# Sums over edges for the first 256 nodes: row fetches from a DRAM table instead of a matrix product with counts

## The chip, the cores and the metric

The kernel runs on one core of a Trainium2 chip. Its time is the device time of one execution in microseconds (us). A time before or after is the median over several executions on the chip; one execution was also recorded by the hardware profiler, and the views below are of that one. Engines are named as the profile names them: PE is TensorE (PEld its loads of weights), DVE is VectorE, ACT is ScalarE, POOL is GpSimd, SP is the engine that starts most of the DMAs. L1773 is line 1773 of the kernel before the change.

## The reference

The input is 3125 nodes with 256 features and 103125 edges, sorted by destination (every node has an edge to itself). Four layers follow one another, each with a layer norm ahead of it and its input added behind it: a graph attention network of three layers, a mixture of experts, a layer that sums messages over edges, and a second mixture of experts. The change is in the third of them:

```python
def _L1_gnn_ref(x, W, M, edge_src, edge_dst):
    self_term = x @ W
    msg = x @ M
    agg = jax.ops.segment_sum(msg[edge_src], edge_dst, num_segments=x.shape[0])
    return jax.nn.relu(self_term + agg)
...
x = x + _L0_gnn_ref(_layernorm(x, axis=-1), src, dst, ...)
x = x + _L0_ffn_ref(_layernorm(x, axis=-1)[None], ...)[0]
x = x + _L1_gnn_ref(_layernorm(x, axis=-1), L1_gnn_W, L1_gnn_M, src, dst)
x = x + _L1_ffn_ref(_layernorm(x, axis=-1)[None], ...)[0]
```

## The kernel before

Nodes lie in 25 tiles of 128 (P is 128, NT is 25, D is 256). Early on, the edge lists are turned into a matrix of counts, 3125 sources by 3125 destinations, as bytes in SBUF. It is kept in 13 groups of destinations (GROUPS): twelve of 256 and a last one of 53. The attention layers and the sum layer all use it, so that a sum over edges becomes a product with the counts.

The attention's second layer also has a second way. For the first 512 destinations (class Apart, L2049) the sources of each node were listed, 38 to a node (OWN); nodes with more edges give the remainder to a shared tile of up to 128 heavy nodes with 20 places each (HEAVY). `ends` holds where each node's list begins and how long it is, `key` says which heavy place a node has, and `who` the source numbers, one column for each place. Each column is one indirect DMA on POOL that fetches 128 rows from a DRAM table (L2168), and DVE adds the rows (L2194). Those columns stand among the steps of the matrix product, at times that were written down by hand (`events`), and the block is issued under `tc.manual_schedule()` (L1526): there each engine takes its instructions in the order in which the code issues them. Elsewhere the scheduler of the framework orders each engine's instructions by a model of their times.

The sum layer is `dense_sum` (L1742). It has two phases.

- **Messages** (L1754 to L1762). In pieces of one to four tiles, `normalised` (L1723) makes the layer norm: statistics on DVE (L1728, L1729), the root on ACT (L1731), the scaling on DVE (L1735), two transposes on PE (L1738) and a copy on ACT into xnT (L1739). PE multiplies with M (L1760), and the message is kept as two numbers of reduced precision whose sum is the exact one: ACT casts the high part (L1761), DVE subtracts it for the rest (L1762).
- **Groups** (L1763 on). For each group of 256 destinations PE goes over 25 tiles of sources. At each of those steps ACT turns the bytes of the counts into numbers (`cr`, L1773, from a pool of four buffers; it also gives the sum of the row into `seen`, which at the end tells whether all edges were counted), and PE multiplies them with both halves of the messages, once for each of the group's two tiles (L1777). At the first step the self term x W is added into the same accumulators (L1780). When a group has ended, `back` finishes it during the next group, from step 8 on: for each tile ACT copies the low half out of PSUM (y, L1785), DVE adds the high half (L1786) and adds the clipped sum to x (L1787); then `normalised` makes the two tiles of xnT for the next layer. `back` stands at step 8 of the code; where its instructions come on each engine is the scheduler's decision, since this phase is not under manual_schedule.

After the sum layer the last mixture begins with the products of xnT (L1056).

Of the kernel before, what the change touches and what calls it, by code (L numbers as in the profile page):

```python
# [10 lines left out]
F32 = mybir.dt.float32  # L11
F16 = mybir.dt.float16
BF16 = mybir.dt.bfloat16
I32 = mybir.dt.int32
# [3 lines left out]
OP = mybir.AluOpType  # L18
# [1261 lines left out]
HELD = 64.0  # L1280

# [76 lines left out]
def dense_attention(tc, dram, counts, x_in, big, ident, eps, layers, src, dst, rows, high, make_router, over, count,  # L1358
# [11 lines left out]
    with tc.tile_pool(name="dw", bufs=1) as cp, tc.tile_pool(name="dwl", bufs=2) as wl, \  # L1370
# [3 lines left out]
        with tc.tile_pool(name="dp", bufs=6) as pmp, tc.tile_pool(name="ds", bufs=2) as sp, \  # L1374
# [12 lines left out]
            apart = Apart(tc, cp, dram, locator, *count, ident, top)  # L1387
# [332 lines left out]
    return expert  # L1720


def normalised(nc, wp, pp, x, t0, n, xnT, ident, eps):  # L1723

    mv = wp.tile([P, n, 2], F32, name="n_mv")
    for i in range(n):
        st = wp.tile([P, 6], F32, name="n_st")
        nc.vector.bn_stats(st, x[:, t0 + i])  # L1728
        nc.vector.bn_aggr(mv[:, i], st)  # L1729
    rstd = wp.tile([P, n], F32, name="n_rstd")  # L1730
    nc.scalar.activation(rstd, mv[:, :, 1], AF.Sqrt, bias=eps)  # L1731
    nc.vector.reciprocal(rstd, rstd)
    for i in range(n):
        xn = wp.tile([P, D], F32, name="n_xn")
        nc.vector.tensor_scalar(xn, x[:, t0 + i], mv[:, i, 0:1], rstd[:, i:i + 1], op0=OP.subtract, op1=OP.mult)  # L1735
        ps = pp.tile([P, KD, P], F32, name="ps_n")
        for k in range(KD):
            nc.tensor.transpose(ps[:, k], xn[:, k * P:(k + 1) * P], ident)  # L1738
        nc.scalar.copy(xnT[:, :, (t0 + i) * P:(t0 + i + 1) * P], ps)  # L1739


def dense_sum(tc, x, xnT, counts, ws, wm, ident, eps, total):  # L1742
# [6 lines left out]
    with tc.tile_pool(name="s1", bufs=1) as cp, tc.tile_pool(name="sb", bufs=4) as bp, \  # L1749
# [4 lines left out]
        msg = cp.tile([P, NT, 2, D], F32R, name="msg")  # L1754
        for t0, n in PIECES:
            normalised(nc, yp, tp, x, t0, n, xnT, ident, eps)
            for t in range(t0, t0 + n):
                ps = mp.tile([P, D], F32, name="ps_m")
                for k in range(KD):
                    nc.tensor.matmul(ps, xnT[:, k, t * P:(t + 1) * P], wm[:, k], start=(k == 0), stop=(k == KD - 1))  # L1760
                nc.scalar.copy(msg[:, t, 0], ps)  # L1761
                nc.vector.tensor_tensor(msg[:, t, 1], ps, msg[:, t, 0].bitcast(F32), op=OP.subtract)  # L1762
        later = []  # L1763
        for a, (c, n) in enumerate(GROUPS):
            edges = counts_of(counts, a)
            tiles = [(q, (c + q) // P, min(P, n - q)) for q in range(0, n, P)]
            n += n % 2
            acc = po.tile([P, 2, 2, D], F32, name="acc")
            for s in range(NT):
                if later and s == 8:  # L1770
                    later.pop()()
# [3 lines left out]
                for j, (q, t, r) in enumerate(tiles):  # L1775
# [3 lines left out]
                    for k in range(KD if s == 0 else 0):  # L1779
                        nc.tensor.matmul(acc[:r, j, 0], xnT[:, k, c + q:c + q + r], ws[:, k], start=False, stop=False)  # L1780

            def back(tiles=tiles, acc=acc):
# [5 lines left out]
                normalised(nc, yp, tp, x, tiles[0][1], len(tiles), xnT, ident, eps)  # L1788
            later.append(back)
        later.pop()()  # L1790
# [258 lines left out]
class Apart:  # L2049

    def __init__(self, tc, cp, dram, locator, before, every, ident, top):
# [3 lines left out]
        self.ends = cp.tile([P, FEW + 1, 2], F32, name="ends")  # L2055
        self.key = cp.tile([P, FEW], F32, name="heavy_key")
        self.width = sum(n for _, n in SLOTS_OF)
        self.who = cp.tile([P, self.width], I32, name="apart_who")
        self.table = dram.tile([N, ROW], F32, name="apart_rows")

    def save(self, sources, t, r):
        self.nc.sync.dma_start(self.table[t * P:t * P + r], sources.h[:r, t])
# [184 lines left out]
def routed(ctx: ExitStack, tc: tile.TileContext, i: dict, out: bass.AP, over):  # L2247
# [12 lines left out]
    with tc.tile_pool(name="counts", bufs=1) as kp:  # L2260
# [7 lines left out]
        expert = dense_attention(tc, dram, counts, i["x"], big, ident, eps, layers, i["src"], i["dst"], (rows0, rows),  # L2268
# [3 lines left out]
        with tc.tile_pool(name="s0", bufs=1) as sp:  # L2272
# [5 lines left out]
            dense_sum(tc, x, xnT, counts, ws, wm, ident, eps, over[:, 2:3])  # L2278
# [94 lines left out]
```

## Time and profile before

| | us |
|---|---|
| median of 14 executions (1865.08 to 1878.02) | 1868.56 |
| the profiled execution | 1870.27 |
| its span, from its first instruction to its last | 1868.5 |
| PE busy, of the span | 1768.1 (95%) |
| DVE busy | 1021.0 (55%) |
| ACT busy | 727.2 (39%) |
| POOL busy | 499.6 (27%) |
| sum layer: branch before it passed, first message product, first whole group, last cr | 1384, 1390, 1422, 1593 |
| products with the counts, L1777, in the layer | 625 of 404 ns, 158 busy |
| row fetches of the attention, L2168 | 172 of 1083 ns, 472 to 753 |

The page of the profile gives the busy time of each engine, the span in 40 slices, the chain of work that ended last, and the costliest groups of instructions. "Chain of waits" is that chain followed back from the last instruction: where an engine ran without waiting, its own work stands there. In the views of waits, "A <- B: 53.5, 17, 6.9" says that A's engine stood idle until B for 53.5 us in total, 17 times, at most 6.9. In a timeline each line has the start, the duration, the engine, the line of the code, the operation, what it writes and reads, its shapes and how many were merged; a bracket gives the idle time just before it and what ended it. Matmuls are pipelined, so one of 404 ns can start every 233 ns. The clock is the share of full speed that PE was granted.

### The profile page before, as it was taken

How to read it: one execution, taken by the hardware profiler on the slowest of the kernel's cores; microseconds unless marked ns; L12 is line 12 of the kernel's file. 1: busy time of each engine (PE TensorE's matmuls, PEld its weight loads, DVE VectorE, ACT ScalarE, POOL GpSimd, SP SyncE). 2: the span in 40 equal slices, each digit the busy share in tenths (PEclk: the TensorE clock that was granted, in tenths of full speed). 3: DMA queues.
4: the chain of work that ended last, by engine and by line, in shares of the span. 5: the costliest groups of instructions: out<-in, count | busy, mean ns of one | idle time of the engine just before them, and what ended most of it. 6: DMA issues, size and time to landing. Idle time of an engine off the chain costs nothing. (4 is left out here: it accounts for less than half of the span.)

```text
span 1868.5 us, 27219 instructions
## 1 busy us (share of the span) xinstructions
PE 1768.1 (95%) x9196; PEld 1379.9 (74%) x9196; DVE 1021.0 (55%) x2933; ACT 727.2 (39%) x2080; POOL 499.6 (27%) x634
## 2 busy tenths in 40 slices
PE   6999999999698988999999999999989999999997
PEld 4788888887586777788887866666668887455786
DVE  6888888875475757677777842222244222333221
ACT  3767667671011111122222331111127999454221
POOL 4210110000566766123333233333310000122121
PEclk9999999999898999999999999999999999999999
DMA  4111213757322332211111176877430000723884
GB/s 116 33 47 49 77 49 149 318 225 283 81 76 79 85 84 74 89 39 46 46 46 42 43 221 185 242 199 197 111 89 1 1 1 1 237 113 151 262 302 125
DMA packets 123716, 215.45 MB, mean 115 GB/s; under 512 B 14811, under 2 KB 86657, under 8 KB 123528
## 3 DMA queue, kind: packets, MB, share of 16 engines
q1 hardware_dynamic: 85860, 137.38, 22.0%
q0 software_dynamic: 24704, 56.84, 11.6%
q10 hardware_dynamic: 12994, 19.29, 3.2%
q8 instruction: 79, 1.29, 0.3%
q14 instruction: 79, 0.65, 0.1%
HBM read 122.54 MB, written 92.61 MB: 115 GB/s over the span
## 5 line engine op out<-in xcount | busy, mean ns | idle before, releaser
L1577 PE MATMUL acc<-big,pm 128*128 128x257 f32 x3400 | 799.7, 386 | 14.9 <-DVE pm L1574 9.5
L1577 PEld LDWEIGHTS acc<-big,pm 128*128 128x128 f32 x3400 | 635.0, 192 | 108.6 <-DVE pm L1574 14.9
L1574 DVE SCALAR_TENSOR_TENSOR pm<-tau,big,counts 128x256 f32<-128x256 f32 (+1 forms) x875 | 403.1, 480 | 123.9 <-PE acc L1577 98.7
L2168 POOL DMA_INDIRECT apart_row<-apart_rows,apart_who x172 | 186.4, 1083 | 104.7 <-issue 44.7
L1777 PE MATMUL acc<-msg,cr 128*128 128x512 f32 (+1 forms) x625 | 157.9, 403 | 0.1
L891 PE MATMUL ps_h<-xsT,w 128*128 128x384 f32 x448 | 147.3, 487 | 0.0
L1777 PEld LDWEIGHTS acc<-msg,cr 128*128 128x128 f32 (+1 forms) x625 | 114.7, 185 | 29.2 <-ACT cr L1773 1.2
L1773 ACT ACTIVATE cr<-counts 128x256 fp32r<-128x256 uint8 (+1 forms) x325 | 130.6, 402 | 13.9 <-PE acc L1777 6.9
L2034 ACT CAST counts<-acc_c 128x500 uint8<-128x500 f32 (+1 forms) x155 | 95.9, 677 | 94.5 <-PE acc_c L2024 94.3
L891 PEld LDWEIGHTS ps_h<-xsT,w 128*128 128x128 f32 x448 | 84.7, 190 | 58.0 <-issue 1.9
L1344 PE MATMUL ps_m<-we,yT 128*128 128x258 f32 (+1 forms) x248 | 72.1, 411 | 35.4 <-issue 24.6
L2009 DVE TENSOR_TENSOR ohk<-iota_k,key 128x2016 f16<-128x2016 f16 (+1 forms) x79 | 94.6, 1198 | 19.8 <-PE acc_c L2024 19.7
L894 ACT ACTIVATE silu<-ps_h 128x384 f32<-128x384 f32 x60 | 29.4, 490 | 170.4 <-PE ps_h L891 160.0
L1475 ACT ACTIVATE yT<-ps_m 128x256 f32<-128x256 f32 (+1 forms) x25 | 9.5, 378 | 218.6 <-PE ps_m L1473 104.9
L2003 ACT ACTIVATE ohs<-iota_s,low 128x128 f16<-128x128 f16 x286 | 94.0, 400 | 0.0
L1056 PE MATMUL ps_H<-big,t_w 128*128 128x512 f32 (+1 forms) x224 | 93.1, 552 | 0.8 <-ACT H L1058 0.5
L895 DVE TENSOR_TENSOR hid<-silu,ps_h 128x384 f32<-128x384 f32 x60 | 33.2, 554 | 104.0 <-PE ps_h L891 104.0
L911 POOL DMA_INDIRECT sums<-y,who x45 | 70.0, 1556 | 74.1 <-DVE y L909 66.1
L1184 PE MATMUL ps_y<-t_wd,hsT 128*128 x384 | 87.1, 379 | 0.4 <-ACT hsT L1232 0.4
L2024 PEld LDWEIGHTS <-ohs 128*128 128x128 f16 x1250 | 77.7, 98 | 10.9
L1344 PEld LDWEIGHTS ps_m<-we,yT 128*128 128x128 f32 (+1 forms) x248 | 45.0, 197 | 53.8 <-issue 28.1
L2024 PE MATMUL acc_c<-ohk,ohs 128*128 128x125 f16 x1250 | 84.5, 218 | 0.0
(424 smaller groups left out, 2246.1 us busy)
## 6 DMA issues: line engine op xcount, KB each, us to landing
rows<-empty SPq DMA_DIRECT2D x16, 2564.0 KB
big<-in_L_ffn_w_dram SPq DMA_DIRECT2D x36, 512.0 KB
w<-in_L_ffn_w_dram ACTq DMA_DIRECT2D x36, 512.0 KB
hs<-rows SPq DMA_DIRECT2D x23, 641.0 KB
rows<-empty SPq DMA_DIRECT2D x16, 516.0 KB
t_wd<-in_L_ffn_Wd_dram SPq DMA_DIRECT2D x8, 1024.0 KB
big<-in_L_ffn_Wd_dram SPq DMA_DIRECT2D x6, 1024.0 KB
xs<-rows SPq DMA_DIRECT2D x14, 387.0 KB
```

Source lines behind the costliest of these rows:

```text
L891: nc.tensor.matmul(ps, w[:, k, j * P:(j + 1) * P], xsT[:, k], start=(k == 0), stop=(k == KD - 1))
L1056: nc.tensor.matmul(ps[:, :n], a[:, k, j * P:(j + 1) * P], xnT[:, k, c:c + n], start=(k == 0), stop=(k == KD - 1))
L1344: nc.tensor.matmul(ps[:r], xT[:, k], w[:, k], start=(k == 0), stop=(k == KD - 1))
L1574: nc.vector.scalar_tensor_tensor(pm[:, :n], tau[:, :n], now.rho[:, of:of + 1], edges[:, of, :n], op0=OP.max, op1=OP.mult)
L1577: nc.tensor.matmul(acc[:r, j, :D + 1], pm[:, q:q + r], now.h[:, of, :D + 1], start=(s == 0), stop=(s == NT - 1))
L1773: nc.scalar.activation(cr[:, :n], edges[:, s, :n], AF.Copy, accum_out=seen[:, a * NT + s:a * NT + s + 1])
L1777: nc.tensor.matmul(acc[:r, j].rearrange("p h d -> p (h d)"), cr[:, q:q + r], msg[:, s].rearrange("p h d -> p (h d)"), start=(s == 0), stop ...
L2003: nc.scalar.activation(far[:, i], self.iota_s, AF.Abs, scale=-1.0, bias=self.low32[:, batch, i:i + 1])
L2009: nc.vector.tensor_tensor(to[:, i:tiles].rearrange("p t (x u) -> p t x u", u=2), iota.rearrange("p (x u) -> p x u", u=2)[:, None].to_broad ...
L2024: nc.tensor.matmul(acc[:, u], ohs[:, i], ohk[:, i, :KEYS], start=(t == 0), stop=(t == TW - 1))
L2034: nc.scalar.copy(to[:, :, d0 % PAIR:d0 % PAIR + whole * WIN].rearrange("p s (u d) -> p u s d", u=whole), acc[:, :whole])
L2168: nc.gpsimd.indirect_dma_start(out=row[:, j], out_offset=None, in_=self.table[:, :], in_offset=bass.IndirectOffsetOnAxis(ap=self.who[:, q ...
```

## The change

Group 0 of the sum layer, 256 destinations in two tiles, no longer goes through the product with the counts. Its sums follow the edges, with the lists that the attention made: `ends`, `key` and `who` are now kept in the pool of the counts (`kp`) until the sum layer has ended.

- Ahead of the messages DVE sums group 0's counts into `seen`, in five reductions; the room of those counts then holds six places for rows, and one-hots of the heavy nodes are made and transposed.
- After each tile's message, POOL adds the two halves and SP stores the row to a DRAM table (`save`).
- After the first of the remaining groups, `begin` issues six fetches. There are 96 in all: 20 columns of the heavy places, then 38 for each of the two tiles. DVE multiplies each row by a mask (`real`) and adds it (`slot`); behind a slot the fetch that is six further on is issued.
- When a tile's columns are done, PE multiplies the one-hots with the heavy sums and adds the self term (`finished`); at steps 19 and 4 `close` adds both, adds the clipped sum to x, and makes xnT.
- From the second remaining group on everything stands under `tc.manual_schedule()`. `back` is in two parts, at step 8 (the y copies, the sums, the statistics, the root and the scaling) and at step 16 (the transposes and the copies). Both are issued ahead of that step's cr.

The constants say at which step a row's sum is written into the order: the first after 8.5 us (ARRIVED), each further one after 1.26 (PACE), with 13.8 for a group (WHOLE), 11.7 for the first (FIRST) and 0.468 for a step (PART).

```diff
+SINGLE = 2
+FOLLOW = SLOTS_OF[:1 + SINGLE]
+PLACES = 6
+BACK, CLOSE = (8, 16), (19, 4)
+ARRIVED, PACE = 8.5, 1.26
+FIRST, WHOLE, PART = 11.7, 13.8, 0.468
...
+def normalised_steps(nc, wp, pp, x, t0, n, xnT, ident, eps):
...
+    for i in range(min(2, n)):
+        scaled(i)
+    yield
     for i in range(n):
-        xn = wp.tile([P, D], F32, name="n_xn")
-        nc.vector.tensor_scalar(xn, x[:, t0 + i], mv[:, i, 0:1], rstd[:, i:i + 1], op0=OP.subtract, op1=OP.mult)
+        if i >= 2:
+            scaled(i)
+        xn = held.pop(0)
         ps = pp.tile([P, KD, P], F32, name="ps_n")
...
+class Followed:
+    def __init__(self, tc, dram, apart, counts, cp, pp, ident):
...
+        for t in range(SINGLE):
+            hot = self.place()[:, :P]
+            nc.vector.tensor_scalar(hot, numbers, apart.key[:, t:t + 1], None, op0=OP.is_equal)
+            nc.tensor.transpose(ps[:, t], hot, ident)
+        nc.scalar.copy(self.back, ps)
...
+    def save(self, t, msg):
+        nc, row = self.nc, self.place()
+        nc.gpsimd.tensor_tensor(row, msg[:, t, 0].bitcast(F32), msg[:, t, 1].bitcast(F32), op=OP.add)
+        nc.sync.dma_start(self.table[t * P:(t + 1) * P], row)
+
+    def fetch(self, q):
+        row = self.place()
+        self.nc.gpsimd.indirect_dma_start(
+            out=row, out_offset=None, in_=self.table[:, :],
+            in_offset=bass.IndirectOffsetOnAxis(ap=self.apart.who[:, q:q + 1], axis=0))
+        return row
+
+    def events(self, finished):
...
+        def slot(q, first):
+            row, real = rows.pop(q), self.real[:, q:q + 1]
+            if first:
+                state["acc"] = self.cp.tile([P, D], F32, name="f_acc", bufs=3)
+                nc.vector.tensor_scalar(state["acc"], row, real, None, op0=OP.mult)
+            else:
+                nc.vector.scalar_tensor_tensor(state["acc"], row, real, state["acc"], op0=OP.mult, op1=OP.add)
+            if q + PLACES < total:
+                rows[q + PLACES] = self.fetch(q + PLACES)
...
-def dense_sum(tc, x, xnT, counts, ws, wm, ident, eps, total):
+def dense_sum(tc, dram, apart, x, xnT, counts, ws, wm, ident, eps, total):
+        for s in range(0, NT, WIN):
+            nc.vector.tensor_reduce(seen[:, s:s + WIN], counts_of(counts, 0)[:, s:s + WIN], AX.X, OP.add)
+        singles = Followed(tc, dram, apart, counts, cp, mp, ident)
...
+                singles.save(t, msg)
...
+        def finished(t, acc, hot, heavy):
+            ps = mp.tile([P, D], F32, name="ps_m")
+            nc.tensor.matmul(ps, hot, heavy, start=True, stop=False)
+            for k in range(KD):
+                nc.tensor.matmul(ps, xnT[:, k, t * P:(t + 1) * P], ws[:, k], start=False, stop=(k == KD - 1))
+
+            def close():
+                nc.vector.tensor_tensor(acc, acc, ps, op=OP.add)
+                nc.vector.scalar_tensor_tensor(x[:, t], acc, 0.0, x[:, t], op0=OP.max, op1=OP.add)
+                yield from normalised_steps(nc, yp, tp, x, t, 1, xnT, ident, eps)
+            steps = close()
+            closing.extend((q, lambda: next(steps, None)) for q in CLOSE)
+
+        begin, made = singles.events(finished)
+        order = ExitStack()
+        for g, (a, (c, n)) in enumerate(list(enumerate(GROUPS))[SINGLE // 2:]):
...
+            if g == 1:
+                begin()
+                order.enter_context(tc.manual_schedule())
             acc = po.tile([P, 2, 2, D], F32, name="acc")
             for s in range(NT):
-                if later and s == 8:
-                    later.pop()()
+                for step in [e for e in later if e[0] == s]:
+                    later.remove(step)
+                    step[1]()
+                if closing and closing[0][0] == s:
+                    closing.pop(0)[1]()
                 cr = bp.tile([P, PAIR], F32R, name="cr")
...
+                while g and made and made[0][0] <= (g, s):
+                    made.pop(0)[1]()
...
-                normalised(nc, yp, tp, x, tiles[0][1], len(tiles), xnT, ident, eps)
-            later.append(back)
-        later.pop()()
+                yield from normalised_steps(nc, yp, tp, x, tiles[0][1], len(tiles), xnT, ident, eps)
+            steps = back()
+            later.extend((q, lambda steps=steps: next(steps, None)) for q in BACK)
+        order.close()
+        while made:
+            made.pop(0)[1]()
+        for _, step in later + closing:
+            step()
```

## The prediction

> **What bounds the stage now.** I read the page's slices first (TensorE at nine tenths or more from 1400 to 1590 us, DMA idle there), then the chain of waits from 1370 to 1660 us, then busy time by stretch, then the timeline of one group. The sum layer's groups are a chain of TensorE work alone:
>
> ```profile
> 1558.32 0.86 PE acc L1780 x4
> 1559.19 0.23 PE acc L1777
> 1559.42 0.86 PE acc L1780 x4
> 1560.28 3.26 PE acc L1777 x14
> 1563.54 0.44 PE ps_n L1738 x4
> 1563.98 8.17 PE acc L1777 x35
> 1572.15 0.86 PE acc L1780 x4
> ```
>
> A group of 256 destinations repeats after 13.83 us (1572.15 - 1558.32): 50 message products at 0.233, eight passes of the self term (1.72), four transposes (0.44). So a step of one source tile is 0.466 us.
>
> ```profile
> 1440.00:1480.00 40.00, 40.00 (x180) 32.58 (x179) 10.36 (x33) 36.66 (x159) 0.00 (x0) 1.00 0.00 1
> 1400.00:1410.00 10.00, 10.00 (x53) 7.99 (x52) 9.54 (x36) 6.39 (x20) 0.00 (x0) 1.00 0.01 2
> ```
>
> Columns: stretch, then busy PE, PEld, DVE, ACT, POOL, clock, DMA share, GB/s. In the groups (first line) ACT is busy 36.7 of 40 us, only 8% short of becoming the bound. While messages are made (second line) DVE is busy 9.5 of 10. What ACT does between its conversions (cr, L1773) is the part that the change touches:
>
> ```profile
> 1572.43 0.35 ACT L1785 COPY y<-acc 128x256 f32<-128x256 f32 x1
> 1573.27 0.37 ACT L1785 COPY y<-acc 128x256 f32<-128x256 f32 x1 [0.49 <-DVE y L1786]
> 1575.55 0.28 ACT L1731 ACTIVATE n_rstd<-n_mv,eps 128x2 f32<-128x2 f32 x1
> 1575.74 0.40 ACT L1773 ACTIVATE cr<-counts 128x256 fp32r<-128x256 uint8 x1
> 1577.21 0.60 PE L1738 MATMUL ps_n<-ident,n_xn 128*128 128x128 f32 x4
> 1577.88 0.63 ACT L1739 COPY big<-ps_n 128x256 f32<-128x256 f32 x2
> ```
>
> From the first y copy to the end of the root is 3.40 us, because seven DVE operations stand between. Today three other cr (at 1573.54, 1574.67, 1575.14) go in between, and a fourth follows the root at once; those feed TensorE. The last two lines are the transposes and the copies that wait for them.
>
> **The parts.** The sum is against the profiled execution, 1870.27 us (span 1868.5, 1.77 outside it), 1.7 above the median of 1868.56.
>
> *(a) One group goes*, 13.83. *(b) TensorE work put back* for its two tiles: the spread of the shared rows, one fp32 256-column product of two passes (0.43), four self passes (0.86), two transposes (0.22) for each tile, and two transposes of the one-hots at the start: 2 x 1.51 + 0.22 = 3.24. Net **-10.6**.
>
> *(c) Ahead of the messages*, DVE gets five sums of group 0's counts (128x1280 uint8 to 128x5). No such row exists. The longest sum over full width is L1792 (325 elements, 0.491), a short one is L241 (32 elements, 0.186); their slope, 1.04 ns an element, makes 1.5 us of 1280, 7.5 for five. Masks and one-hots add 1.0 (L2110: 0.28 each). They stand first on DVE, are ready after the branch (1383.96), and statistics come behind them. Before the first 1.4 us and before the second another 1.4 DVE only waits for the loads, so 8.5 - 2.8 = **+5.7** arrives at the messages, where DVE has no slack. Bounds: 0 (placed in the idle time after 1415) to 8.5.
>
> *(d) The table.* 25 additions on POOL (L1545: 0.73 for the same shape, 18 us over a phase of 33) and 25 SP stores at 0.34 to issue, 8.5 us. POOL and SP have nothing else to do here. The last row is fetched only after the last store has landed, some 4.3 us after its issue (466.9 to 471.3 in the attention stage): **0**; without that cover, about 4.
>
> *(e) 96 fetches and 96 sums.* POOL issues one per 1.26 us (0.96 and 0.30), 121 us in all; the first row lands near 1430, the last near 1553, with the stage ending at 1593 or later. 96 sums at 0.40 a piece (starts of L2194 back to back) are 38 us on a DVE that is busy 10 of 40. Six places cover a landing of 3 us. **0**, up to +16 if rows come at the 1.63 us that the attention stage needed a row on average (751.8 - 472.1 over 172): then 156 us, and the end waits.
>
> *(f) Order of issue.* From the second group on, each engine keeps the order of the code. That code puts y copy, y copy and root at step 8 ahead of cr 8, and the two xnT copies at step 16 ahead of cr 16. The cr pool has four buffers, so when ACT reaches step 8 TensorE ends step 3. ACT then: cr 7 (0.46), copies and root (3.40 today with DVE free to reorder, some 3.6 in order), cr 8 until its sum is read (0.51): 4.6 us, against 4 x 0.466 = 1.87 that TensorE can live on. **Wait 2.7 us.** Behind the root stand all later cr, and TensorE waits for those. At step 16 no lead is possible at all: the copy needs the transposes and cr 16 stands behind the copy. From the transposes' start 1.30 to the end of the copies (1577.21 to 1578.51), 0.51 for cr, less 0.60 of transposes: **1.2**. Lead returns during the next self term. Ten full groups x 3.9 = 39, and 4 in the short last one, where the reserve is 4 x 0.26: **+43**. Bounds: 0 if ACT is not held, 55 if DVE is behind with row sums.
>
> *(g) The two followed tiles' closing*, at steps 19 and 4: root 0.3, transposes and copy 1.0, and 1.0 of lead lost for the following step 8, twice: **+4.6**; bounds 0 and 8.
>
> *(h) The clock.* Waits of that size have a second price in this trace:
>
> ```profile
> 581.08:584.49 3.41, 1.34 (x6) 0.87 (x5) 2.84 (x8) 0.00 (x0) 2.49 (x4) 1.00 0.34 90
> 584.49:587.90 3.41, 2.79 (x8) 1.66 (x6) 0.68 (x2) 0.00 (x0) 2.50 (x4) 0.50 0.39 109
> ```
>
> TensorE idled 2.07 us in the first stretch, and the next was granted half a clock. A wait of 2.29 (to 702.55) had the same follow, one of 2.95 (to 545.33) had none. Two of three, 11 waits, 1.7 us lost in 3.41 at half clock: **+11** to 12; I take 11, bounds 0 and 19.
>
> On this the Trainium skill, "TensorE: Matmul & The Clock Gate", Part 1, says that half rate is what an idle window of about 3.4 us brings. By it a wait of 2.7 would halve nothing and the sum would be 11 lower; the row disagrees, and the row decides.
>
> **Sum:** -10.6 + 5.7 + 43 + 4.6 + 11 = +53.7, so 1924 in a profiled execution and **1922** against the median. By the bounds of c, f, g and h at their likely sides (f 25 to 50, h 0 to 19) this case reaches from 1895 to 1945.
>
> **A precedent in the same trace.** The second attention layer keeps the order of issue too, with 172 row fetches. Its groups, by the reciprocal L1622, take 30.9 us on average (490.28 to 768.01, nine groups) and those of the third layer 23.82. In its waits from 515 to 770 us
>
> ```profile
> DVE lr L1351 <- ACT raw L1480: 53.5, 17, 6.9
> POOL apart_row L2168 <- DVE apart_acc L2194: 39.4, 20, 8.7
> ```
>
> DVE stood 17 times for 3.1 us behind an ACT result, and POOL waited for DVE, not for rows: order costs there, and fetches do not.
>
> **Rivals.**
>
> 1. *ACT is not held* (faster). If ACT still runs ahead at steps 8 and 16, only a to c remain: 1868.6 - 10.6 + 5.7 = 1864, or 1858 if the counts' sums are hidden. For it: ACT has 2 us to spare in a group, and y could start earlier. Against it: those 2 us cannot be used through four buffers, and L1351's waits show that order is kept. It decides where the wait per group falls below (10.6 - 5.7)/11 = 0.45 us. 0.22.
> 2. *Only the long step is partly held* (slower by less): DVE runs the statistics while ACT waits and the clock stays up; f of 10 to 25 and h of 0 give 1872 to 1895. 0.10.
> 3. *Rows set the pace.* If DVE waits for rows ahead of step 8, the root comes later by as much, and the groups go at the pace of 11 rows. At 1.63 a row that is 18 us a group, no more than case f has already; it adds to f only if rows need over 1.7 us. Together with half clocks throughout: 1945 to 1980. 0.06.
> 4. *The change saves nothing and costs nothing*, f near 5 (0.45 a group): within 0.2%, 3.7 us, about what a measurement of this kernel can tell from no change. 0.04.
>
> The likeliest, held ACT, has 0.58. The range 1862 to 1945 takes it in with case 2, case 4 and the half of case 1 that ends at 1862 to 1865; left out are 0.11 below and 0.08 above. Faster 0.22, same 0.04, slower 0.74.
>
> **What would show it.** Right: in the chain, groups 17 to 19 us apart instead of 13.83; in the waits, TensorE's loads for acc waiting some 2.5 us for cr once a group and about 1 for the copies; ACT's root waiting some 2.5 us for DVE's n_mv; clocks of 0.5 between 1440 and 1640; five sums of about 1.5 on DVE from 1384 and the first transposes 5 us later; fetches 1.26 us apart in bursts, POOL waiting for DVE between. Wrong: groups of 13.8 with ACT's cr between the y copies, which is case 1; or DVE waiting for DMA ahead of the row sums, which is case 3.

## The result and the profile after

The changed kernel takes 1966.88 us (median of 13, 1955.16 to 1974.53); the kernel before took 1869.88 beside it (62 executions). The ratio is 1.0513, 95% interval 1.0494 to 1.0531: slower by 97 us where 53 were forecast. The profiled execution is 1967.0, its span 1965.3 (1868.5 before).

One thing has to be said for the runs below. The kernel before takes 1863 to 1870 us on some chips and 1811 to 1815 on others. I call them kind A and kind B. The two traces of the prediction and of the result are of kind A; each set of experiments ran on one chip, two sets on kind A and three on kind B.

**Where the time went.** Two stretches of the sum layer: the *message stage*, from the first edge copy (cr) to that of the second group, and the *group stage*, from there to the last sum over `seen`.

| us | before | changed | |
|---|---|---|---|
| message stage | 48.4 (1383.9 to 1432.3) | 55.5 (1385.6 to 1441.1) | +7.1 |
| group stage | 160.9 (to 1593.2) | 247.3 (to 1688.4) | +86.4 |
| all else of the span | 1659.2 | 1662.5 | +3.3 |

The group stage has one whole group less: 160.9 - 13.8 = 147.1 would be left, so 100 us are new in it. The chain of waits of the changed kernel, in a group with fetches and in one behind the last fetch:

```profile
1472.36 0.86 PE acc L1906 x4
...
1474.78 2.06 issue
1476.84 1.70 PE acc L1903 x2
...
1484.71 3.95 PE acc L1903 x16
...
1490.02 4.41 PE acc L1903 x18
...
1494.94 0.86 PE acc L1906 x4
...
1497.35 2.08 issue
...
1656.55 0.86 PE acc L1906 x4
...
1666.03 3.95 PE acc L1903 x16
...
1671.34 4.64 PE acc L1903 x19
1675.98 1.00 PE acc L1906 x4
```

The self term (L1906) opens a group: 22.6 us from 1472.36 to the next, 19.4 at the end of the layer, 13.83 before. Both have a gap between their first products and those at 1484.71 and 1666.03: there the chain goes through ACT and DVE, from the y copies (L1913) to the root. Only the first has "issue" just behind the self term: TensorE waits 2 us for nothing that the profile shows. The busy time by stretch (columns as in the prediction), while messages are made, in the groups with fetches, and behind the last:

```profile
1400.00:1410.00 10.00, 9.85 (x47) 7.61 (x45) 8.71 (x34) 4.51 (x15) 4.51 (x6) 0.91 0.20 67
1500.00:1520.00 20.00, 15.03 (x47) 10.54 (x46) 8.86 (x22) 10.72 (x47) 8.69 (x10) 0.74 0.21 59
1640.00:1660.00 20.00, 16.41 (x74) 12.91 (x72) 6.02 (x18) 11.88 (x54) 0.00 (x0) 1.00 0.01 1
```

In the second line PE starts 47 operations in 20 us, in the third 74, and 90 before. The step at which `back` stands, which before let three cr in between, now looks like this:

```profile
1480.72 0.35 ACT L1913 COPY y<-acc 128x256 f32<-128x256 f32 x1
...
1481.56 0.37 ACT L1913 COPY y<-acc 128x256 f32<-128x256 f32 x1 [0.49 <-DVE y L1914]
...
1483.96 0.29 ACT L1742 ACTIVATE n_rstd<-n_mv,eps 128x2 f32<-128x2 f32 x1 [2.03 <-DVE n_mv L1740]
1484.17 0.40 ACT L1899 ACTIVATE cr<-counts 128x256 fp32r<-128x256 uint8 x1
...
1484.71 0.72 PE L1903 MATMUL acc<-msg,cr 128*128 128x512 f32 x2 [1.09 <-ACT cr L1899]
```

ACT stands 2.03 us before the root, and no cr is made from the first y copy to the root's end, 3.53 us: the wait that the prediction worked out. The waits of the layer (1383 to 1700) show a second kind beside it:

```profile
DVE y L1914 <- ACT y L1913: 90.5, 9, 13.4
POOL counts L1797 <- DVE f_acc L1823: 77.5, 35, 13.0
...
ACT cr L1899 <- PE acc L1903: 39.3, 43, 2.3
...
DVE f_acc L1823 <- DMA counts<-sum_rows,apart_who: 29.4, 39, 1.1
...
ACT n_rstd L1742 <- DVE n_mv L1740: 26.9, 16, 2.0
...
PE acc L1903 <- issue: 22.2, 10, 5.1
...
ACT cr L1899 <- remote: 13.8, 8, 5.8
```

DVE is early, not late: it waits 90.5 us for the y copies. But TensorE waits 22.2 us for nothing seen ("issue"), and ACT 13.8 us for a sender that the view doesn't name ("remote"). No step of the prediction had these two. ACT also waits 43 times for TensorE to release a cr buffer; of that the run with plain loads below, which has no such loss, keeps 20.4 us in 27 waits. In the timeline of ACT and PE (operations of DVE and POOL and the loads left out), behind the opening of a group:

```profile
1496.04 0.42 ACT L1899 ACTIVATE cr<-counts 128x256 fp32r<-128x256 uint8 x1 [1.66 <-remote]
...
1496.61 0.75 PE L1903 MATMUL acc<-msg,cr 128*128 128x512 f32 x2
...
1498.87 0.42 ACT L1899 ACTIVATE cr<-counts 128x256 fp32r<-128x256 uint8 x1 [2.31 <-PE acc L1903]
...
1499.43 0.73 PE L1903 MATMUL acc<-msg,cr 128*128 128x512 f32 x2 [2.08 <-issue]
1501.01 0.42 ACT L1899 ACTIVATE cr<-counts 128x256 fp32r<-128x256 uint8 x1 [1.63 <-PE acc L1903]
```

One step, two products, takes 2.1 to 2.8 us there where 0.466 is usual, and no DVE result is waited for. In this stretch POOL sends fetches every 1.26 us.

### The profile page after: what moved, and what is told of

It is laid out like the page before. It is cut to its first block, busy times and chain, and to the rows that moved or that the text cites. A ratio compares the mean times of both kernels' runs of the same rounds, so it can differ in the third digit from the quotient of the medians.

```text
span 1965.3 us, 27520 instructions
## 1 busy us (share of the span) xinstructions
PE 1796.1 (91%) x9152; PEld 1387.9 (71%) x9152; DVE 1078.0 (55%) x3040; ACT 711.7 (36%) x2030; POOL 609.2 (31%) x756
## 5 line engine op out<-in xcount | busy, mean ns | idle before, releaser
L1903 PE MATMUL acc<-msg,cr 128*128 128x512 f32 (+1 forms) x575 | 174.0, 452 | 64.6 <-ACT cr L1899 36.8
L2301 POOL DMA_INDIRECT apart_row<-apart_rows,apart_who x172 | 184.9, 1075 | 105.3 <-DVE apart_acc L2327 48.4
L1899 ACT ACTIVATE cr<-counts 128x256 fp32r<-128x256 uint8 (+1 forms) x300 | 117.7, 396 | 67.2 <-PE acc L1903 39.3
L1797 POOL DMA_INDIRECT counts<-sum_rows,apart_who x96 | 92.7, 966 | 107.9 <-DVE f_acc L1823 77.5
L894 ACT ACTIVATE silu<-ps_h 128x384 f32<-128x384 f32 x60 | 29.4, 490 | 170.6 <-PE ps_h L891 168.5
```

Source lines behind the costliest of these rows:

```text
L1797: self.nc.gpsimd.indirect_dma_start(out=row, out_offset=None, in_=self.table[:, :], in_offset=bass.IndirectOffsetOnAxis(ap=self.apart.who[ ...
L1899: nc.scalar.activation(cr[:, :n], edges[:, s, :n], AF.Copy, accum_out=seen[:, a * NT + s:a * NT + s + 1])
L1903: nc.tensor.matmul(acc[:r, j].rearrange("p h d -> p (h d)"), cr[:, q:q + r], msg[:, s].rearrange("p h d -> p (h d)"), start=(s == 0), stop ...
L2301: nc.gpsimd.indirect_dma_start(out=row[:, j], out_offset=None, in_=self.table[:, :], in_offset=bass.IndirectOffsetOnAxis(ap=self.who[:, q ...
```

## The experiments

The group stage is read in each, since a kernel whose sums are left out gives other rows to the mixture behind, which then takes another time (43 us more in the run with the order alone). All group stages of this table have ten whole groups and the short one. Of g1, g2, g3, h1 and h2 the whole is one execution, else a median.

| run | kind | message stage | group stage | whole, and before beside it |
|---|---|---|---|---|
| changed (result) | A | 55.5 | 247.3 | 1966.9 / 1869.9 |
| e5_changed | A | 55.7 | 243.8 | 1960.5 / 1869.0 |
| e1_scheduler_order | B | 55.1 | 210.9 | 1869.0 / 1815.2 |
| e2_order_alone | B | 55.1 | 205.8 | 1906.9 / 1815.2 |
| e3_order_sums | B | 55.5 | 205.3 | 1863.9 / 1815.2 |
| e4_order_fetches | B | 55.3 | 206.0 | 1865.4 / 1815.2 |
| e6_spread | A | 55.5 | 204.3 | 1916.7 / 1869.0 |
| e7_no_counts | A | 52.4 | 244.5 | 8686.5 / 1869.0 |
| f1_order_alone | A | 55.6 | 208.4 | 1960.3 / 1863.3 |
| f2_order_fetches | A | 55.7 | 298.4 | 2012.5 / 1863.3 |
| f3_order_sums | A | 55.8 | 205.4 | 1918.4 / 1863.3 |
| f4_direct | A | 55.5 | 206.0 | 1920.9 / 1863.3 |
| g1_narrow | B | 55.3 | 205.9 | 1903.9 / 1815.0 |
| g2_half | B | 55.0 | 205.8 | 1866.5 / 1815.0 |
| g3_spread_direct | B | 55.3 | 152.1 | 1809.4 / 1815.0 |
| g4_spread_late | B | 55.8 | 154.0 | 1814.8 / 1815.0 |
| h1_narrow | B | 55.0 | 205.8 | 1905.5 / 1811.4 |
| h2_few_saves | B | 53.9 | 206.8 | 1908.6 / 1811.4 |

### Order, sums and fetches apart (kind B)

The order goes:

```diff
             if g == 1:
                 begin()
-                order.enter_context(tc.manual_schedule())
```

> The changed kernel without its order of issue for the groups: fetches, row sums, counts and masks stay, and the instructions of the groups are ordered as they were in the kernel before. Two theories are weighed here and in the next three runs. Theory A, the order: the ScalarE queue that holds the copies and the root of one group ahead of the next group's edge copies costs everything. It expects the whole of the excess over the message sums to go, so about 1866 to 1880 us. Theory B, the fetches: in the changed kernel's trace the groups after the last fetch take 19.2 us and those with fetches 22 to 29 us, and a step of the products whose operands are there takes 2.1 to 2.8 us instead of 0.47 while POOL issues fetches. It expects the slow steps to stay and only the 5.4 us of each group that the order costs (19.2 against 13.83) to go, so about 1967 - 54 = 1913 us, 1900 to 1925.

No fetches, and only the first row product of each sum:

```diff
         row = self.place()
-        self.nc.gpsimd.indirect_dma_start(...)
         return row
...
             if first:
                 state["acc"] = self.cp.tile([P, D], F32, name="f_acc", bufs=3)
                 nc.vector.tensor_scalar(state["acc"], row, real, None, op0=OP.mult)
-            else:
-                nc.vector.scalar_tensor_tensor(state["acc"], row, real, state["acc"], op0=OP.mult, op1=OP.add)
```

> The changed kernel with its order of issue, but no row is fetched and only the first row product of each sum is left: the followed sums are of whatever lies in the places, so their part of the output is left out. Theory A (the order) expects nearly no gain: the time stays over 1950 us. Theory B (the fetches) expects each of the ten groups in order to take what the last ones of the changed kernel take, 19.2 us, so about 1870 - 10.6 for the group left out + 10 in the message stage + 10 x 5.4 for the order + 3 for its closing = 1927 us, 1915 to 1940.

The first half of that diff alone:

> The changed kernel with its order and all 96 row sums on VectorE, but no row is fetched: the sums are of whatever lies in the places. It tells the row sums (0.48 us each, 46 us in all) from the fetches. Theory A expects over 1950 us, theory B the time of the run with the order alone plus at most 10 us, and a third, C, that VectorE's row sums and not the fetches slow the steps, the changed kernel's 1967 us less at most 10.

The second half alone:

> The changed kernel with its order and all 96 fetches, but only the first row product of each sum: the others are left out, so VectorE's row sums cost nothing and no fetch waits for VectorE. The fetches should then follow each other at their pitch of 1.26 us, 121 us in all, over some six groups. Theory B expects the groups beside them to take 23 to 29 us and the time to stay at 1950 to 1975 us; theories A and C expect that it doesn't matter that rows arrive: A the time of the run with the order alone and of the changed kernel to be one (over 1950 us for both), C the time of the run with the order alone, some 1927 us.

Measured, in this order: ratios to before of 1.030 (1.0283 to 1.0317), 1.051 (1.0492 to 1.0527, with the 43 us of the mixture in it), 1.027 (1.0253 to 1.0287) and 1.0282 (1.026 to 1.0305). The group stage takes 205.3 to 206.0 us in the three runs in order: neither the sums alone nor the fetches alone cost anything here, though the fetches ran at full pace beside the groups. Busy time by stretch of the run with order and fetches:

```profile
1380.00:1400.00 20.00, 16.40 (x74) 13.08 (x72) 3.60 (x11) 14.05 (x64) 15.13 (x17) 1.00 0.39 105
```

17 fetches, 105 GB/s, and PE goes on as in the groups behind the last fetch of the changed kernel (74 operations). This was against theory B, which wanted 1950 us and more from this run; but the kernel before was 55 us faster here than I knew it, and the changed kernel itself had not been run there, so this settled nothing yet.

The run without the order fits neither theory. Its five groups with fetches take 21.6 to 29.4 us and the later ones 13.7 to 15.0, but PE doesn't wait for "issue" in it. Here the scheduler put some ten row sums, each behind its row, ahead of one group's y add:

```profile
1446.83 0.95 POOL L1797 DMA_INDIRECT counts<-sum_rows,apart_who  x1 [0.30 <-issue]
1447.16 0.48 DVE L1823 SCALAR_TENSOR_TENSOR f_acc<-counts,f_real,f_acc 128x256 f32<-128x256 f32 x1 [0.75 <-DMA counts<-sum_rows,apart_who]
1447.56 0.42 DVE L1913 TENSOR_TENSOR y<-acc,y 128x256 f32<-128x256 f32 x1
1448.02 0.37 ACT L1912 COPY y<-acc 128x256 f32<-128x256 f32 x1 [12.79 <-DVE y L1913]
...
1448.85 0.79 PE L1902 MATMUL acc<-msg,cr 128*128 128x512 f32 x1 [11.51 <-ACT cr L1898]
```

The second y copy waits 12.79 us for the first y add, and behind it stand the cr that PE needs. So dropping the order swaps one wait for another.

### The same chip for before and after (kind A)

> The kernel before, unchanged, for its trace beside the others. In the first four experiments the kernel before took 1815 us and not 1870, and the attention layer with row fetches (to 762.2 us in the trace shown first) ended 56 us earlier in them than in that trace. If that comes with the chip, this run shows one of the two: 1815 us with that layer ending near 706 us, or 1870 us with it ending near 762.

> The changed kernel, unchanged, beside the kernel before on one chip, because the four experiments ran where the kernel before takes 1815 us. Theory D, the slow fetch state: fetched rows slow TensorE's steps only where the kernel before takes 1870 us (its attention layer with fetches takes 56 us longer there). It expects here, if the kernel before is at 1815 us, the group stage of the run with the order alone, that is 17.8 to 21 us a group and about 1815 + 50 = 1865 us; if it is at 1870 us, 1967 us as before. Theory E, fetches and sums together: rows fetched while VectorE sums them slow the steps on any chip. It expects 22 to 29 us for the groups with fetches and a ratio near 1.05 in either place.

Both repeated what was measured first (1869.3 us, and a ratio of 1.0521, 1.0487 to 1.0555), so these two speak only for the place; they leave D and E open.

The closing of a group in six parts:

```diff
-BACK, CLOSE = (8, 16), (19, 4)
+BACK, CLOSE = (3, 6, 10, 13, 16, 19), (21, 23, 1, 4)
...
+    yield
     rstd = wp.tile([P, n], F32, name="n_rstd")
...
             nc.tensor.transpose(ps[:, k], xn[:, k * P:(k + 1) * P], ident)
+        yield
         nc.scalar.copy(xnT[:, :, (t0 + i) * P:(t0 + i + 1) * P], ps)
...
                 for j, (q, t, r) in enumerate(tiles):
+                    if j:
+                        yield
                     y = yp.tile([P, D], F32, name="y")
```

> The changed kernel with the closing of a group cut into six parts at steps 3, 6, 10, 13, 16 and 19 instead of two at 8 and 16 (and that of a followed tile into four): one output copy, the other with the statistics, the root with the scaling, the first transposes, the first copy with the second transposes, the second copy. Each ScalarE instruction so stands some three steps behind what it waits for. If the 4 to 7 us that a group takes over 13.83 in the run with the order alone are ScalarE's waits for VectorE and TensorE in the order (2.0 us for the root, 1.5 to 3.2 for the transposes, and TensorE's restart), the groups without fetches fall to 14 to 15 us: 40 to 55 us less than the changed kernel where the slow fetch state is absent, so a ratio to before of 0.995 to 1.005. If the order costs something else, it gains less than 15 us.

The ratio falls to 1.0264 (1.0233 to 1.0296), 44 us less than the changed kernel beside it; the expected 0.995 to 1.005 was for a place without the slow state, and this was kind A. The last two groups take 14.6 and 14.2 us. Those with fetches still take 15.5 to 29.5.

The count sums go:

```diff
-        for s in range(0, NT, WIN):
-            nc.vector.tensor_reduce(seen[:, s:s + WIN], counts_of(counts, 0)[:, s:s + WIN], AX.X, OP.add)
+        nc.vector.memset(seen[:, :NT], 0.0)
```

> The changed kernel without the five count sums of group 0 (their part of the count check is left out, set to zero); the masks, saves, fetches and row sums stay. From its first edge copy to that of the second group the changed kernel takes 55.5 us against 48.4 before. If the sums ahead of the statistics cause it, as the prediction had it, this stage falls by 5 to 7 us; if the saves or the masks do, by less than 2.

The message stage falls from 55.7 to 52.4, 3.3 us. That is nearer to "the sums" than to "not the sums", but below the 5 to 7 that I wanted. (The whole of 8687 us is the fallback that the kernel runs when the total of the counts doesn't give the number of edges.)

### Order, sums, fetches and plain loads (kind A)

> The run with the order alone once more (no row fetched, only the first row product of each sum; that part of the output is left out), because it ran where the kernel before took 1815 us, and the changed kernel itself has only been seen where it takes 1870 us. Read by its stage of the groups, from the second group's first edge copy to the last sum (in the changed kernel on the later chip 1430.4 to 1674.2, 243.8 us; in the first run with the order alone 205.8 us). With no fetches theory D (a state in which fetched rows slow TensorE's steps) and theory E (fetches and sums together) both expect 203 to 210 us here too; if it takes 235 us or more, the order itself costs more on such a chip and neither holds.

> The run with order and fetches once more, without the row sums behind the first of each (that part of the output is left out): 96 fetches follow each other at 1.26 us over some 121 us. Where the kernel before takes 1815 us its stage of the groups took 205.9 us, the same as the order alone. Theory D expects here, where the kernel before takes 1870 us, that the groups beside the fetches take 23 to 30 us, and the stage 230 to 260 us; theory E expects 203 to 210 us, since nothing is summed.

> The run with order and row sums once more, without fetches (the sums are of whatever lies in the places). Both theories expect what the order alone takes, 203 to 210 us in the stage of the groups; a longer stage would put the loss on VectorE's sums.

```diff
         row = self.place()
-        self.nc.gpsimd.indirect_dma_start(
-            out=row, out_offset=None, in_=self.table[:, :],
-            in_offset=bass.IndirectOffsetOnAxis(ap=self.apart.who[:, q:q + 1], axis=0))
+        t = q % NT
+        self.nc.sync.dma_start(row, self.table[t * P:(t + 1) * P])
```

> The changed kernel with a plain load of 128 rows in their order on SyncE's queue in place of each fetch by list on GpSimd's: as many bytes into the same places, the same row sums waiting for them (so the followed sums are of other rows). If it is the bytes that slow TensorE's steps, the groups take 22 to 29 us as in the changed kernel and the stage of the groups some 244 us; if it is the fetch by list (its descriptors, its 256-byte or 1024-byte rows one by one, GpSimd's part), the stage falls to 203 to 212 us.

Order alone 208.4, with sums 205.4, with sums and plain loads 206.0, with fetches by list and no sums **298.4**. Theory D holds: the fetches by list alone make the loss beyond the order, on this kind of chip. A falls as the whole cause (the order alone is 35 to 39 us short of the changed kernel on the same kind, though it makes some 60 of the 100 us), and so do C and E (the sums have no part in it). The size was not foreseen: 230 to 260 us were expected for the stage, and 23 to 30 for a group beside fetches; three groups take 40.7, 55.2 and 53.5 us. The one between the first two takes 20.3, since POOL pauses there for the first product of the next sum. The same stretch of code that ran at x74 on kind B, in busy time by stretch of the run with order and fetches on kind A:

```profile
1500.00:1520.00 20.00, 3.29 (x9) 1.27 (x7) 0.00 (x0) 1.53 (x6) 15.13 (x17) 0.65 0.37 105
...
1660.00:1680.00 20.00, 16.40 (x73) 13.01 (x73) 3.60 (x11) 14.37 (x66) 0.00 (x0) 1.00 0.01 2
```

POOL sends the same 17 fetches, the transfers move the same 105 GB/s, and PE does 9 operations. Behind the last fetch (second line) it is back at 73. Its timeline shows what the wait is:

```profile
1503.56 0.95 POOL L1797 DMA_INDIRECT counts<-sum_rows,apart_who  x1 [0.31 <-issue]
...
1511.21 0.42 ACT L1897 ACTIVATE cr<-counts 128x256 fp32r<-128x256 uint8 x1 [7.92 <-remote]
...
1511.78 1.22 PE L1901 MATMUL acc<-msg,cr 128*128 128x512 f32 x2 [7.70 <-issue]
1512.36 0.96 POOL L1797 DMA_INDIRECT counts<-sum_rows,apart_who  x1 [0.30 <-issue]
...
1523.67 0.95 POOL L1797 DMA_INDIRECT counts<-sum_rows,apart_who  x1 [0.30 <-issue]
1524.50 0.42 ACT L1897 ACTIVATE cr<-counts 128x256 fp32r<-128x256 uint8 x1 [12.77 <-remote]
...
1525.06 1.22 PE L1901 MATMUL acc<-msg,cr 128*128 128x512 f32 x2 [12.06 <-issue]
```

ACT's cr waits 7.92 and 12.77 us, PE's products follow it by 0.57, and POOL's fetches keep their 1.26 us throughout. The view names no sender, but the trace holds one: both cr wait for a semaphore that PE alone raises, at the end of a step's second product. It rose at 1511.13 and 1524.41, 0.08 us ahead of the cr. PE's last products before had started at 1503.69 and 1512.37 and would have ended at 1504.08 and 1513.00, so the signals came at least 7.1 and 11.4 us late. In the run with plain loads the signal follows the product's end by 0.01 to 0.02 us at each wait of over half a microsecond. So what is late is TensorE's own product or its signal, not POOL, DVE or a landing; which of the two can't be told, because the ends of products are modelled. Nor is code being loaded: from 1500 to 1520 us the transfers are those of the fetches' queue alone,

```profile
q0 software_dynamic: 768, 2.10, 36.9%
```

while the two queues of the kind "instruction" have lines of their own wherever they move anything. The plain loads carry as many bytes into the same places (102 GB/s) and leave PE alone:

```profile
1440.00:1460.00 20.00, 16.41 (x74) 12.87 (x73) 10.90 (x27) 12.91 (x60) 0.00 (x0) 1.00 0.35 102
```

### What of a fetch, and what of the order (kind B)

Rows of 64 columns in the run with order and fetches:

```diff
-        self.table = dram.tile([NP, D], F32, name="sum_rows")
+        self.table = dram.tile([NP, D // 4], F32, name="sum_rows")
...
-            out=row, out_offset=None, in_=self.table[:, :],
+            out=row[:, :D // 4], out_offset=None, in_=self.table[:, :],
```

> The run with order and fetches (no row sums but the first of each; that part of the output is left out) with rows of 64 columns in place of 256: as many fetches and rows, a quarter of the bytes. Where the kernel before takes 1870 us, wide rows made the stage of the groups 298 us and the order alone 208. If the bytes or the time that the rows occupy the transfers are the cause, it falls to 205 to 230 us; if the count of rows or GpSimd's part of a fetch is, it stays over 270 us. If the kernel before takes 1815 us here, it says nothing (206 us either way).

Half of the fetches in the changed kernel (`if q % 2: return row` ahead of the fetch):

> The changed kernel with every second fetch left out (the place keeps what it had, and its row sum stays; the followed sums are wrong in part): 48 fetches, about twice as far apart. The changed kernel's stage of the groups took 244 and 247 us, the order alone 208. If each fetch costs TensorE a fixed time, half the excess stays, 224 to 230 us; if the loss sets in only when fetches follow each other closely, it goes nearly whole, 205 to 215 us.

Both landed on kind B and tell nothing, as the first expectation said for that case: 205.9 and 205.8, the order's own.

The edits of the spread closing and of the plain loads together:

> The closing of a group in six parts, with plain loads in place of the fetches by list (the followed sums are of other rows): the order's cost without what slows the steps. If the 4 to 7 us a group of the order are ScalarE's waits, every group takes 14 to 15 us as the last ones of the run with the spread closing did (14.6, 14.2), so the stage of the groups takes 150 to 160 us in place of 206; if some other cost of the order is left, over 170.

The group stage falls to 152.1 us, in the expected 150 to 160; against 206.0 with plain loads and the closing at two steps (on kind A; order and sums on kind B took 205.3), 54 us are the price of that closing: ACT's waits and the half clock behind them, which no group has here. Groups take 13.8 to 15.2.

The spread closing, with the masks made behind the messages (the lines of `numbers`, `real` and `back` in a method `masks` that is called there):

> The changed kernel with the closing in six parts and with the masks and their transposes made behind the messages instead of ahead of them; the count sums stay ahead. The message stage (first edge copy to that of the second group) takes 55.5 us, 52.4 without the count sums, 48.5 in the kernel before. If the masks hold ScalarE and TensorE there (the copy of the masks waits 6.9 us for them), it falls by 2 to 4 us; if the saves make the rest, it stays within 1 us of 55.5. The whole: 1905 to 1917 us where the kernel before takes 1870, so a ratio of 1.019 to 1.026, still slower than before because the fetches slow the steps; 1805 to 1820 us, a ratio near 1, where it takes 1815.

The ratio is 0.9997 (0.9987 to 1.0006): the same as before, with the whole result, all 96 fetches and all sums. PE is busy throughout, beside 106 GB/s of fetches and behind them:

```profile
1420.00:1440.00 20.00, 20.00 (x92) 15.84 (x91) 12.46 (x32) 18.11 (x85) 15.43 (x16) 1.00 0.37 106
...
1500.00:1520.00 20.00, 20.00 (x93) 16.60 (x92) 9.24 (x28) 15.38 (x71) 0.00 (x0) 1.00 0.03 8
```

The message stage stays at 55.8, so the masks aren't in it. What the group stage gains, 160.9 - 154.0 = 6.9, the message stage gives back, 55.8 - 48.4 = 7.4 (the stages of the kernel before are those of kind A; its layer has no fetches). On kind A the spread closing was at 1.0264, so no version with the whole result beats the kernel before.

### Narrow rows again, and the saves (kind B)

> The narrow rows once more (order and 96 fetches of 64 columns in place of 256, no row sums but the first of each; that part of the output is left out), because the first such run was where the kernel before takes 1815 us and the fetches cost nothing. Where it takes 1870 us, wide rows made the stage of the groups 298 us and the order alone 208: 205 to 230 us if the bytes are the cause, over 270 us if the count of rows or GpSimd's part of a fetch is.

Kind B once more, 205.8: it tells nothing, and the question stays open.

Saves of the first six tiles only (`if t < PLACES: singles.save(t, msg)`):

> The run with the order alone (no fetches, only the first row product of each sum, that part of the output left out) with the saves of 6 of the 25 message tiles only. The message stage, from the first edge copy to that of the second group, takes 55.1 to 55.8 us in every run with the count sums, 52.4 without them, 48.5 in the kernel before, and moving the masks did not change it (55.8). If the saves on GpSimd slow VectorE or the stage's end, it falls by 3 to 4 us; if not, it stays within 0.5 us of 55.5 and the rest is the half clock and the order that the scheduler makes of the stage.

The message stage is 53.9, against 55.1 in the run of the order alone on kind B, one trace of each: 1.2 us for 19 of 25 saves, between the two expectations and less than the 3 to 4 for which the saves alone would stand.

## Why the prediction was wrong, by its steps

*(a), (b), one group less, and TensorE's work put back:* right. With neither ACT's waits nor slow steps the group stage takes 152.1 us against 147.1 for one group less, and of these 5.0 the two tiles were to cost 3.2 on TensorE.

*(c) +5.7 ahead of the messages:* +7.1, within its bounds. The first message product stands 11.3 us behind the first cr, 6.3 before the change and 6.5 without the count sums, so at the start of the stage they cost 4.8. The sums took what the slope gave:

```profile
L1856 DVE TENSOR_REDUCE seen<-counts x5: 1476/1477/1487, 1385.6 to 1391.2; 128x5 f32<-128x1280 uint8 x5
```

(minimum, median and maximum in ns). Taken away they give 3.3 us of the whole stage back. The masks give nothing, 19 of the saves 1.2; for all 25 that makes some 1.6 as an estimate. About 2 us are not accounted for. At the start of the stage the clock is halved for 13.65 us (6.83 before the change, 10.24 without the sums), and no run separates what that costs.

*(d) Table 0:* it costs those 1.2 to 1.6.

*(e) 96 fetches and 96 sums 0, at most +16:* **this is the step that failed.** The sums and their rows cost nothing, as said (205.4 with sums, 208.4 without): once a sum had begun, DVE waited for rows 29.4 us in all, at most 1.1 at a time, and it was early for y. But the fetches by list cost 247.3 - 206.0 = 41 us of group stage (38 in the repeat; the plain loads ran on another chip of kind A), by a way that the step didn't have: not through rows that come late, but through products of TensorE whose signals come late while fetches are under way, so that ACT and the next products stand still. With POOL unhindered it is 298.4 - 208.4 = 90 us. I looked for work that hides the fetches on POOL, DVE and the transfers, and for whether they would slow others I looked at nothing.

*(f), (g), (h), the order, two closings and the half clock:* right in sum. With b they were 43 + 4.6 + 11 + 3.2 = 62; the group stage with plain loads is 206.0 - 147.1 = 59 over. The stretch from the first y copy to the root's end was put at 3.6 and is 3.53 (eight operations of DVE lie in it before the change, not seven); the spread closing, which takes away those waits and with them the half clock, takes away 54 us. In the run with plain loads the clock is halved six times for 3.41 us in the groups, 20.5 us and so about 10 lost; 11 was said. In the changed kernel it was halved for 64.8 us, since the slow steps leave TensorE idle as well.

*The precedent* was read the wrong way round. From DVE's 53.5 us behind ACT and POOL's 39.4 behind DVE I took that "order costs there, and fetches do not". But who held ACT? In the same waits of the kernel before (515 to 770 us) stood:

```profile
ACT yT L1475 <- PE ps_m L1473: 88.0, 12, 16.1
...
ACT yT L1475 <- remote: 39.2, 4, 14.8
```

The first of these is no sign of a loss: on kind B the same layer, here in the trace of the spread closing with late masks (470 to 710 us), has more of it. What it lacks is the second, and most of DVE's wait behind ACT:

```profile
ACT yT L1481 <- PE ps_m L1479: 156.9, 21, 17.4
...
DVE lr L1357 <- ACT raw L1486: 15.9, 19, 1.7
```

On kind A the repeat of the kernel before (470 to 760 us) has 98.0 us of "remote" and 49.3 of DVE behind ACT. The semaphore behind "remote" is again one that PE alone raises. On kind B the nine groups take 24.9 us (488.3 to 712.4 in the run without the order) against 30.9, beside 23.8 in the third layer: of the 7.1 us that I gave to the order, 6.0 go with the kind of chip, and by what the fetches do in the sum layer I take them for the fetches'; no run took the fetches out of this layer. The 55 us between the two kinds in the kernel before are mostly this layer: from the first trace to that of the run without the order it ends 56 us earlier.

*The rivals.* ACT was held, so the first falls; on kind B, with the closing spread, its kind of time (1814.8 against 1815.0) is reached, with 13.7 to 15.3 us a group. The third, rows that set the pace, has the time that was measured in its 1945 to 1980, but by luck: DVE did wait for rows ahead of its sums, which was named as its sign, yet DVE was not what the groups waited for. Its condition, over 1.7 us a row, looked at the rows and not at TensorE. *What was to show it:* the root's wait (2.03 for some 2.5), the halved clock and the sums were seen as said; the groups were 19 to 30 us apart and not 17 to 19.

## What to carry to other kernels

A transfer that is hidden behind other engines can still slow them: before pricing it at nothing, compare the pace of TensorE's steps with and without such transfers in the trace at hand, and follow a chain of waits to its end, "remote" and "issue" included. Under an order of issue, put an instruction of a busy queue several steps behind what it waits for; here that alone took the group stage from 206 us to 152. And measure both kernels on one chip before comparing an experiment with either.

## What the runs showed of the hardware

- **Fetches by list and TensorE.** 96 indirect fetches of 128 rows of 1 KB at one per 1.26 us stretched the group stage from 208.4 to 298.4 us on a chip of kind A and left it at 206.0 on one of kind B (205.8 for the order alone), with the same 105 GB/s. As many bytes by plain loads: 206.0 on kind A. In an unbroken stretch of 38 fetches (1487.2 to 1533.7) ACT's waits for TensorE grew from 1.6 us at 1500.67 to 12.8 at 1524.50; the two that followed were 5.1. The Trainium skill, "SBUF — State Buffer", section "Who interferes with whom", says that "DMA never contends with a compute engine"; the run of 298.4 us speaks against that as a rule, since on that chip TensorE was slowed beside DMAs, by whatever way. What of a fetch does it, its rows, their descriptors or POOL's part, stays open, since both runs with narrow rows were on kind B. Whether the kind belongs to the chip or to the hour does too: each chip was used in one set. The changed kernel itself was not run on kind B.
- **The half clock.** The Trainium skill, "TensorE: Matmul & The Clock Gate", Part 1, puts half rate behind an idle window of about 3.4 us. In the run with plain loads a window didn't have to be idle throughout. Cut into windows of 3.41 us that begin where the halved stretches begin, its groups have six with 2.1 to 3.2 us of idle TensorE, all followed by half a clock, and six with 1.3 to 1.9, none of them followed by it. In the changed kernel's groups the eleven windows at full clock with 2.06 us or more were followed by it, those with up to 1.59 were not. One pair of the first run:

```profile
1508.56:1511.97 3.41, 1.31 (x6) 1.08 (x7) 2.91 (x10) 2.05 (x10) 0.00 (x0) 1.00 0.00 0
1511.97:1515.38 3.41, 3.41 (x10) 2.65 (x9) 3.20 (x8) 1.65 (x8) 0.00 (x0) 0.50 0.67 195
```
